# A graph attention layer: which engine loads the last chunks of a quad row by row, and what these loads wait on

## The chip, the core and the metric

The kernel runs on one NeuronCore of a Trainium2 chip. The metric is device time in microseconds (us), as the median of several executions. One further execution was recorded by the hardware profiler; the traces below are from that one.

## What is computed

A graph attention layer over 12,500 nodes with 128 features and 200,000 edges sorted by their target, with 4 heads of 32 values each:

```python
h   = relu(layernorm(x))                        # (12500, 128)
hn  = (h @ W_node.T).reshape(N, 4, 32)
e   = (edge_attr @ W_edge.T).reshape(E, 4, 32)
att = sum(concat([hn[src], hn[tgt], e], -1) * a, -1)   # one score per edge and head
att = where(att > 0, att, 0.2 * att)
m   = maximum(segment_max(att, tgt), 0)
ex  = exp(att - m[tgt])
denom = segment_sum(ex, tgt) + (E - deg)[:, None] * exp(-m)
out = x + segment_sum((ex / denom[tgt])[:, :, None] * hn[src], tgt).reshape(N, 128)
```

The costly access is `hn[src]`: for every edge a row is fetched by the index of its source, and the sources are random.

## The kernel before

**Tiling.** The edges stand in 392 groups of 512 slots (slot 0 of a group carries the sum over from the group before). A group has four chunks of 128 edges, one edge to a partition. Four groups make a quad; there are 98 quads. Quads are joined to "supers": 2 and 2 at the start, 4 in the middle, 3, 3, 2, 2, 2, 2 at the end. A softmax is made once per super.

**The table.** A first stage (until some 97 us) normalizes the nodes, multiplies them by the weights and writes a table to HBM: one row of 137 floats (548 bytes) per node, with the node's values, a one for the count and its scores as a source. Meanwhile GpSimd already gathers raw inputs for the first quads.

**The gathers.** `gather` (L137 to L151) makes one indirect DMA on GpSimd (L149) for each chunk: 128 rows of the table, by the indices in `srci`, to `ga`, a buffer for eight quads. A gather of quad q overwrites what quad q-8 left, so it waits for the matmuls that read that. The gathers of quad q+2 stand in the program at the start of the logits of quad q.

**Chunks by row.** Some chunks aren't gathered on GpSimd. `by_row` (L134) lists quads whose last chunk (group 3, chunk 3) is loaded by ScalarE instead, with 128 separate DMAs of one row each, whose address is taken from a register (`loaded_by_row`, L703 to L725). The registers are loaded from a tile `at_row` of byte offsets, which VectorE makes (L715) from the sources `of` (L708, a load issued by SP), 12 registers at a time (`windows`, L498, a TENSOR_LOAD in the trace). `load_rows` issues a number of these rows at given places: from the sums of quad 6 on, five behind the copy of the count (L756) and one behind the copy of the sums (L759) of each group, so 24 a quad. When the logits of such a quad begin, ScalarE copies the finished tile to `ga` (L870).

**Logits** (`all_logits`, `logits`). For each group VectorE marks which target each edge has (`at`, L558, from the targets `db`), and PE adds the targets' scores (L564, from the windows `pw`) and the edges' (L567, from the features `ea`). Per quad VectorE then adds the sources' scores from the gathered rows (`U`, L588): the first use of a quad's gathers.

**Sums** (`sums`, `complete`, `complete_group`). For each group VectorE weighs the gathered rows (L813) and makes a matrix of marks (L826), and PE sums by target (L833). Then a serial step follows: VectorE scales the sum that runs over from the group before (L752), ScalarE copies its count (L756), PE adds chunk 0 (L758), ScalarE copies the result from PSUM (`pt`, L759). That copy is waited for by L752 of the group after. `divide` (L856, L860) makes the output of a quad, with the inputs `xw`.

**SP's queue.** SP issues the loads `ea` (L310), `db` (L315), `dr` (L540) and, through `issue` (L512), `pw`, `xw` and the stores of the results, in the program's order; an instruction that waits holds all behind it.

**Order.** The order on each engine is written by hand: `together` takes a step of each of several generators in turn. The logits run four to five quads ahead of the sums in mid-kernel, less at the end. The waits are put in by the framework. A DMA issued from SP or ScalarE takes one of eight semaphores (shared by both) and, before it is issued, waits until the DMA that held that semaphore last has landed.

Of the kernel before, what the change touches and what calls it, by code (L numbers as in the profile page):

```python
# [8 lines left out]
F32 = mybir.dt.float32  # L9
BF16 = mybir.dt.bfloat16  # L10
I32 = mybir.dt.int32
# [4 lines left out]
P = 128  # L16
# [10 lines left out]
J = 4  # L27
# [4 lines left out]
QG = 4  # L32
# [18 lines left out]
def kernel(  # L51
# [79 lines left out]
    ga_all = consts.tile([P, QUADS, QG, J, ROW], F32, name="ga")  # L131
    GA, GATHERED = {}, set()
    whole = lambda g: E - g * NE + 1 >= GE
    by_row = [ROWS_FROM + ROWS_AHEAD - -(k + 1) * P // ((BEHIND_COUNT + BEHIND_SUMS) * QG) for k in range(nq)]  # L134
    by_row = [q for q in by_row if q < nq and quads[q][1] == QG and whole(quads[q][0] + QG - 1)]
    is_by_row = lambda q, i, j: q in by_row and (i, j) == (QG - 1, J - 1)

    def gather(q, rows, width, lo, hi):

        g0, m = quads[q]  # L140
        ga = GA[q] = ga_all[:, q % QUADS]
        for i in range(lo, hi):
            n = -(-min(E - (g0 + i) * NE + 1, GE) // P)
            if n < J:
                nc.vector.memset(ga[:, i, n:, :], 0.0)
            for j in range(n):
                if is_by_row(q, i, j):
                    continue
                nc.gpsimd.indirect_dma_start(  # L149
                    out=ga[:, i, j, 0:width], out_offset=None, in_=rows,  # L150
                    in_offset=bass.IndirectOffsetOnAxis(ap=srci[:, g0 + i, j:j + 1], axis=0))  # L151
# [323 lines left out]
    with tc.tile_pool(name="work", bufs=2) as work, \  # L475
# [20 lines left out]
        def windows(of, size, g, n, engine=mybir.EngineType.SP):  # L496

            return nc.values_load_multi_w_load_instructions(  # L498
                of[0:1, g:g + n], engines=[engine], min_val=0, max_val=(N - 1) * size,
                skip_runtime_bounds_check_because="a node's row")[1]  # L500
# [7 lines left out]
        def issue(*kinds, all_of=False):  # L508

            for kind in kinds:  # L510
                for _ in range(len(due[kind]) if all_of else min(1, len(due[kind]))):
                    nc.sync.dma_start(*due[kind].pop(0))  # L512
# [187 lines left out]

        ROW_TILES = {}

        def loaded_by_row():  # L703

            def sources_of(q):
                g = quads[q][0] + QG - 1
                of = work.tile([1, P], I32, name="of")
                nc.sync.dma_start(of, src.rearrange("(o e) -> o e", o=1)[:, (g + 1) * GE - P:(g + 1) * GE])  # L708
                return of

            of = sources_of(by_row[0]) if by_row else None
            yield
            for k, q in enumerate(by_row):
                at_row = work.tile([1, P], I32, name="at_row")
                nc.vector.tensor_scalar(at_row, of, float(4 * ROW), None, op0=OP.mult)  # L715
                tile_q = work.tile([P, ROW], F32, name="by_row")
                for p in range(P):
                    if p == P // 2 and k + 1 < len(by_row):
                        of = sources_of(by_row[k + 1])
                    if p % LOADED == 0:  # L720
                        at = windows(at_row, 4 * ROW, p, min(LOADED, P - p), mybir.EngineType.Activation)
                    nc.scalar.dma_start(as_bytes(tile_q[p:p + 1, :]),  # L722
                                        rows_at(table, at[p % LOADED], 4 * ROW, 1))
                    if p == P - 1:
                        ROW_TILES[q] = tile_q  # L725
                    yield

        def load_rows(q, n):

            for _ in range(n if q >= ROWS_FROM else 0):  # L730
                next(row_steps, None)

        row_steps = loaded_by_row()
        next(row_steps)

        begun, divisions = [], []
        state = {}
# [9 lines left out]
        def complete_group(q, i, ga, hot, pt, acc, fc):  # L747
            g0, m = quads[q]
            g = g0 + i
            if g:  # L750
                before = state["before"]
                nc.vector.tensor_tensor(  # L752
                    ga[0:1, i, 0, 0:H * HW].rearrange("p (h w) -> p h w", w=HW),
                    before[WIN:WIN + 1, 0:H * HW].rearrange("p (h w) -> p h w", w=HW),
                    fc.unsqueeze(2).to_broadcast([1, H, HW]), op=OP.mult)
                nc.scalar.copy(ga[0:1, i, 0, R_CNT:R_CNT + 1], before[WIN:WIN + 1, R_CNT:R_CNT + 1])  # L756
                load_rows(q, BEHIND_COUNT)
            nc.tensor.matmul(acc, hot[:, i, 0, :], ga[:, i, 0, :], start=False, stop=True)  # L758
            nc.scalar.copy(pt[:, i, :], acc)  # L759
            state["before"] = acc  # L760
            load_rows(q, BEHIND_SUMS)
# [28 lines left out]
        def sums(q):  # L790

            for k in range(nq - 3, nq) if q == nq - 3 else [q] if q < nq - 3 else []:
                fetch_inputs(k)
            if q == nq - 4:
                issue("inputs", all_of=True)
            g0, m = quads[q]
            s = of_quad[q]
            s0, sm = groups(s)
            ga = GA.pop(q)
            heads = lambda t: t[:, :, 0:sm * H].rearrange("p j (h g) -> p j h g", h=H)  # L800
            ex, xs, facs = XS[s]
# [64 lines left out]
        def all_logits(q):  # L866
            flush()
            open_logits(q)
            if q in by_row:
                nc.scalar.copy(GA[q][:, QG - 1, J - 1, :], ROW_TILES.pop(q))  # L870
            for i in range(QG):
                logits(q, i)
                issue("weights")
                if i == QG - 1 and q + 2 < nq:
                    issue("weights", all_of=True)
                    fetch_targets(q + 2)
                yield
            state["logits"] = q

# [306 lines left out]
```

## Time and profile before

| what | us |
|---|---|
| median of 3 runs (1998.55 to 2002.2) | 2000.3 |
| the profiled execution | 2004.14 |
| its span, first to last instruction | 2002.4 |
| PE busy, of the span | 1386.6 |
| VectorE busy | 1326.1 |
| ScalarE busy | 420.0 |
| GpSimd busy | 1499.5 |

A row of a group reads: line, engine, operation, what it writes and reads, count; then busy us, mean ns of one; then the idle time of the engine ahead of these instructions and what ended it. In a timeline a row is start us, us, engine, instruction, count, and in brackets the engine's idle time before. "PEld" is the loading of weights in PE, "q" behind an engine's name its sequencer, which issues DMAs and loads registers; these aren't counted as busy.

### The profile page before, as it was taken

The numbers are of one execution on the slowest core, as the hardware profiler recorded it, in microseconds if no ns is written. First come the engines' busy times: TensorE is split into PE (matmuls) and PEld (weight loads), VectorE is DVE, ScalarE is ACT, GpSimd is POOL, SyncE is SP. The second block draws the span as 40 slices with busy tenths as digits, with TensorE's granted clock in tenths as the row PEclk, the third lists the DMA queues.
The fourth block names the chain that finished last, engine by engine and source line by source line (L and its number), as shares of the span: only waits on it lengthen the run. The fifth ranks groups of instructions, "written<-read, shape, count | busy, mean of one in ns | idle before, by whom it ended". The sixth has DMA issues, their size and how long they took to land.

```text
span 2002.4 us, 31260 instructions
## 1 busy us (share of the span) xinstructions
PE 1386.6 (69%) x7327; PEld 1243.7 (62%) x7327; DVE 1326.1 (66%) x3281; ACT 420.0 (21%) x1547; POOL 1499.5 (75%) x1594
## 2 busy tenths in 40 slices
PE   6577877777766757666757675666675766667876
PEld 5567776666665656556656565656564666667775
DVE  6676775776775765655747655656575566667886
ACT  6664111111111111111111111111111111111222
POOL 7777777777777777777777777777777777777774
PEclk8777555555555555555555555555555555555557
DMA  7655765555555554545554555555545565555541
GB/s 252 205 145 118 179 156 134 148 150 150 143 134 140 139 147 123 146 124 135 134 144 125 145 131 131 132 144 124 148 123 144 123 147 127 135 134 139 140 113 37
DMA packets 197514, 279.78 MB, mean 140 GB/s; under 512 B 81544, under 2 KB 146967, under 8 KB 189488
## 3 DMA queue, kind: packets, MB, share of 16 engines
q1 hardware_dynamic: 142158, 165.56, 30.8%
q0 software_dynamic: 49632, 108.56, 23.3%
q10 hardware_dynamic: 5538, 3.64, 0.7%
q8 instruction: 61, 1.00, 0.2%
q14 instruction: 125, 1.02, 0.2%
HBM read 254.26 MB, written 23.30 MB: 139 GB/s over the span
## 4 chain that ended last, share of the span: by engine, by line
DVE 26%; DMA 21%; PE 18%; issue 12%; POOL 11%; ACT 6%; ACTq 4%; SPq 1%; DVEq 0%; POOLq 0%
POOL ga L149 11%; DMA ga<-table,srci 8%; PE acc L833 8%; DVE at L558 4%; PE lg L567 4%; DVE res L860 3%; DMA by_row<-table 3%; ACTq L722 3%; DVE res L856 3%; DMA db<-in_dst_dram 2%; DMA pw<-side 2%; DVE ga L752 2%; DMA ea<-in_edge_t_dram 2%; PE acc L758 2%; DVE ga L813 2%
## 5 line engine op out<-in xcount | busy, mean ns | idle before, releaser
L149 POOL DMA_INDIRECT ga<-table,srci x1479 | 1412.5, 955 | 453.4 <-issue 387.9
L833 PE MATMUL acc<-ga,hot 128*97 128x137 f32 x2352 | 644.4, 445 | 222.0 <-ACT ga L806 184.4
L833 PEld LDWEIGHTS acc<-ga,hot 128*97 128x97 f32 x2352 | 513.4, 276 | 242.4 <-ACT ga L806 195.3
L567 PE MATMUL lg<-wblk,ea 128*128 128x8 f32 x1568 | 405.1, 356 | 0.0
L564 PEld LDWEIGHTS <-at 80*128 80x128 bf16 x1568 | 209.1, 163 | 281.3 <-DVE at L558 259.8
L567 PEld LDWEIGHTS lg<-wblk,ea 128*128 128x128 f32 x1568 | 377.5, 306 | 0.0
L759 ACT COPY pt<-acc 97x137 f32<-97x137 f32 x392 | 107.4, 274 | 1009.9 <-DMA by_row<-table 540.9
L752 DVE TENSOR_TENSOR ga<-acc,facs 1x132 f32<-1x132 f32 x391 | 115.8, 296 | 301.9 <-ACT pt L759 293.7
L564 PE MATMUL lg<-pw,at 80*128 80x12 bf16 x1568 | 169.7, 181 | 210.5 <-DVE at L558 206.4
L758 PE MATMUL acc<-ga,hot 128*97 128x137 f32 x784 | 262.3, 437 | 23.4 <-ACT ga L756 21.5
L558 DVE TENSOR_TENSOR at<-const_ps,db 80x512 bf16<-80x512 f32 x392 | 267.4, 683 | 5.9
L813 DVE TENSOR_TENSOR ga<-ga,ex_ps 128x528 f32<-128x528 f32 x392 | 268.6, 685 | 0.6 <-DVE st L576 0.3
L758 PEld LDWEIGHTS acc<-ga,hot 128*97 128x97 f32 x784 | 190.9, 277 | 44.2 <-ACT ga L756 41.9
L588 DVE TENSOR_TENSOR U<-st,ga 128x64 f32<-128x64 f32 x98 | 26.4, 270 | 243.3 <-DMA ga<-table,srci 213.1
L826 DVE TENSOR_TENSOR hot<-const_ps,slot 128x320 f32<-128x320 f32 x384 | 183.6, 478 | 0.0
L756 ACT COPY ga<-acc 1x1 f32<-1x1 f32 x391 | 59.9, 153 | 193.9 <-DVE ga L752 186.4
L149 POOL DMA_INDIRECT ga<-in_x_dram,srci x72 | 69.1, 959 | 23.1 <-issue 19.8
L856 DVE TENSOR_TENSOR res<-pt,const_ps 80x512 f32<-80x512 f32 (+2 forms) x103 | 67.7, 657 | 4.1 <-DMA pw<-side 0.3
L860 DVE TENSOR_TENSOR res<-res,xw 80x512 f32<-80x512 f32 (+2 forms) x100 | 67.0, 670 | 3.5
L680 PE MATMUL ex_ps<-ident,ex 64*128 64x64 f32 (+2 forms) x112 | 18.2, 310 | 65.6 <-ACT ex L667 65.6
L680 PEld LDWEIGHTS ex_ps<-ident,ex 64*128 64x128 f32 (+2 forms) x112 | 13.4, 202 | 68.3 <-ACT ex L667 68.2
L406 PE MATMUL row_ps<-wcat,hT 128*128 128x137 f32 x198 | 41.4, 361 | 19.3 <-DVE tgt L412 10.0
(139 smaller groups left out, 1041.6 us busy)
## 6 DMA issues: line engine op xcount, KB each, us to landing
db<-in_dst_dram SPq DMA_DIRECT2D x98, 640.0 KB
ea<-in_edge_t_dram SPq DMA_DIRECT2D x98, 512.0 KB
by_row<-table ACTq DMA_DIRECT2D x1920, 0.5 KB
ga<-table,srci POOLq DMA_INDIRECT x1479
xw<-in_x_dram SPq DMA_DIRECT2D x392, 40.0 KB
out_dram<-res SPq DMA_DIRECT2D x392, 40.0 KB
pw<-side SPq DMA_DIRECT2D x392, 1.9 KB
table<-row SPq DMA_DIRECT2D x9, 616.5 KB
```

The lines of the kernel that those rows point to most:

```text
L149: nc.gpsimd.indirect_dma_start(out=ga[:, i, j, 0:width], out_offset=None, in_=rows, in_offset=bass.IndirectOffsetOnAxis(ap=srci[:, g0 + i, ...
L558: nc.vector.tensor_tensor(at[:, i, :], node_ps[0:SPAN, g0 + i:g0 + i + 1].to_broadcast([SPAN, GE]), db[:, i, :], op=OP.is_equal)
L564: nc.tensor.matmul(lg[:, i, j].rearrange("p k h -> p (k h)"), at[:, i, j * P:(j + 1) * P], sw, start=i + j == 0, stop=False, skip_group_ch ...
L567: nc.tensor.matmul(lg[:, i, 2 * w:2 * w + 2, 0, :], ea[:, i, w, :], wblk, start=False, stop=True, skip_group_check=True)
L752: nc.vector.tensor_tensor(ga[0:1, i, 0, 0:H * HW].rearrange("p (h w) -> p h w", w=HW), before[WIN:WIN + 1, 0:H * HW].rearrange("p (h w) -> ...
L758: nc.tensor.matmul(acc, hot[:, i, 0, :], ga[:, i, 0, :], start=False, stop=True)
L759: nc.scalar.copy(pt[:, i, :], acc)
L813: nc.vector.tensor_tensor(val, val, weight.unsqueeze(3).to_broadcast([P, J, H, HW]), op=OP.mult)
L826: nc.vector.tensor_tensor(hot[:, i, :, 0:SPAN], lane_ps.unsqueeze(1).to_broadcast([P, J, SPAN]), slot[:, g, :].unsqueeze(2).to_broadcast([ ...
L833: nc.tensor.matmul(acc, hot[:, i, j, :], ga[:, i, j, :], start=j == 1, stop=False)
L856: nc.vector.tensor_tensor(res[:, :n, :].rearrange("p g (h d) -> p g h d", d=HD), val[:, :, :, 0:HD], share_ps[0:R, :n, :].unsqueeze(3).to_ ...
L860: add.tensor_tensor(res[:, :n, :], res[:, :n, :], xw, op=OP.add)
```

## The change

The rows loaded by ScalarE are 28 a quad instead of 24: after the last group of a quad's sums four more are issued, and the registers are loaded 28 at a time, once per 28 rows. SP loads rows too, 20 a quad, for chunk 2 of group 3 of its own list of quads: three behind each step of the logits and two behind each step of the sums, from quad 2 on, with registers loaded 20 at a time. The list of chunks by row has 31 entries instead of 15. Row tiles have three buffers. Each row DMA adds to one of three semaphores per list that belong to these rows alone, and is left out of the framework's eight; before ScalarE copies a finished tile to `ga`, it waits for the count of that tile's rows.

```diff
-ROWS_FROM, ROWS_AHEAD = 6, 9
-BEHIND_COUNT, BEHIND_SUMS, LOADED = 5, 1, 12
+ROWS_FROM, ROWS_AHEAD, ROW_BUFS = 6, 7, 3
+BEHIND_COUNT, BEHIND_SUMS, BEHIND_QUAD = 5, 1, 4
+SYNC_FROM, BEHIND_LOGITS, BEHIND_HOT = 2, 3, 2
...
-    by_row = [ROWS_FROM + ROWS_AHEAD - -(k + 1) * P // ((BEHIND_COUNT + BEHIND_SUMS) * QG) for k in range(nq)]
-    by_row = [q for q in by_row if q < nq and quads[q][1] == QG and whole(quads[q][0] + QG - 1)]
-    is_by_row = lambda q, i, j: q in by_row and (i, j) == (QG - 1, J - 1)
+    by_row = {}
+
+    def rows_for(a_quad, j, soonest):
+        for k in range(nq):
+            q = soonest - -(k + 1) * P // a_quad
+            if q < nq and quads[q][1] == QG and whole(quads[q][0] + QG - 1):
+                by_row[q, QG - 1, j] = k
+        return a_quad, j
+
+    scalar_rows = rows_for((BEHIND_COUNT + BEHIND_SUMS) * QG + BEHIND_QUAD, J - 1,
+                           ROWS_FROM + ROWS_AHEAD)
+    sync_rows = rows_for((BEHIND_LOGITS + BEHIND_HOT) * QG, J - 2, SYNC_FROM + 6)
...
-                    if p % LOADED == 0:
-                        at = windows(at_row, 4 * ROW, p, min(LOADED, P - p), mybir.EngineType.Activation)
-                    nc.scalar.dma_start(as_bytes(tile_q[p:p + 1, :]),
-                                        rows_at(table, at[p % LOADED], 4 * ROW, 1))
+                    if p % a_quad == 0:
+                        at = windows(at_row, 4 * ROW, p, min(a_quad, P - p), kind)
+                    row = engine.dma_start(as_bytes(to[p:p + 1, :]),
+                                           rows_at(table, at[p % a_quad], 4 * ROW, 1))
+                    row.then_inc(arrived[k % ROW_BUFS], 16)
+                    tc.no_tile_sem_insts.add(row.ins.name)
+                    tc.add_to_no_dep_group(f"rows{q}_{i}_{j}", row.ins)
...
+        def load_rows(steps, q, n):
+            for _ in range(n if q >= (ROWS_FROM if steps is by_scalar else SYNC_FROM) else 0):
+                next(steps, None)
+
+        def take_rows(q):
+            for i, j in [at[1:] for at in by_row if at[0] == q]:
+                to, arrived, count = ROW_TILES.pop((q, i, j))
+                nc.scalar.wait_ge(arrived, count)
+                taken = nc.scalar.copy(GA[q][:, i, j, :], to)
...
+        by_scalar = loaded_by_row(nc.scalar, mybir.EngineType.Activation, *scalar_rows)
+        next(by_scalar)
+        by_sync = loaded_by_row(nc.sync, mybir.EngineType.SP, *sync_rows)
+        next(by_sync)
...
+            if i == m - 1:
+                load_rows(by_scalar, q + 1, BEHIND_QUAD)
...
                 issue("inputs", "results", *(["inputs"] * 3 if q == nq - 3 else []))
+                load_rows(by_sync, q, BEHIND_HOT)
...
-            if q in by_row:
-                nc.scalar.copy(GA[q][:, QG - 1, J - 1, :], ROW_TILES.pop(q))
+            take_rows(q)
...
+                load_rows(by_sync, q, BEHIND_LOGITS)
```

More of the change, by code (lines that the diff above doesn't have):

```diff
@@ L146, in gather @@
             for j in range(n):
-                if is_by_row(q, i, j):
+                if (q, i, j) in by_row:
                     continue
@@ L701, with loaded_by_row, sources_of @@
         ROW_TILES = {}
[L703 to L708, printed above, removed]
+        def loaded_by_row(engine, kind, a_quad, j):
+            chunks = [(q, i) for q, i, c in by_row if c == j]
+            arrived = [tc.alloc_semaphore(f"rows_{j}_{b}") for b in range(ROW_BUFS)]
+            def sources_of(q, i):
+                e = (quads[q][0] + i) * GE + j * P
+                of = work.tile([1, P], I32, name=f"of{j}")
+                nc.sync.dma_start(of, src.rearrange("(o e) -> o e", o=1)[:, e:e + P])
@@ L709, in sources_of @@
                 return of
-            of = sources_of(by_row[0]) if by_row else None
+            of = sources_of(*chunks[0]) if chunks else None
             yield
-            for k, q in enumerate(by_row):
-                at_row = work.tile([1, P], I32, name="at_row")
+            for k, (q, i) in enumerate(chunks):
+                at_row = work.tile([1, P], I32, name=f"at_row{j}")
                 nc.vector.tensor_scalar(at_row, of, float(4 * ROW), None, op0=OP.mult)
-                tile_q = work.tile([P, ROW], F32, name="by_row")
+                to = work.tile([P, ROW], F32, name=f"by_row{j}", bufs=ROW_BUFS)
@@ L717, in loaded_by_row @@
                 for p in range(P):
-                    if p == P // 2 and k + 1 < len(by_row):
-                        of = sources_of(by_row[k + 1])
-                    if p % LOADED == 0:
-                        at = windows(at_row, 4 * ROW, p, min(LOADED, P - p), mybir.EngineType.Activation)
-                    nc.scalar.dma_start(as_bytes(tile_q[p:p + 1, :]),
-                                        rows_at(table, at[p % LOADED], 4 * ROW, 1))
+                    if p == P // 2 and k + 1 < len(chunks):
+                        of = sources_of(*chunks[k + 1])
@@ L724, in loaded_by_row @@
+                    if p % a_quad == 0:
[5 more added lines that the diff above has]
+                    tc.add_to_no_dep_group(f"rows{q}_{i}_{j}", row.ins)
                     if p == P - 1:
-                        ROW_TILES[q] = tile_q
+                        ROW_TILES[q, i, j] = to, arrived[k % ROW_BUFS], 16 * P * (k // ROW_BUFS + 1)
@@ L726, in loaded_by_row @@
                     yield
[L728 to L734, printed above, removed]
+        def load_rows(steps, q, n):
[6 more added lines that the diff above has]
+                taken = nc.scalar.copy(GA[q][:, i, j, :], to)
+                tc.declare_no_dep(taken.ins, group=f"rows{q}_{i}_{j}",
+                                  reason="a semaphore counts the rows of this chunk")
+                tc.declare_fence(taken.ins, group=f"rows{q}_{i}_{j}")
@@ L756, in complete_group @@
                 nc.scalar.copy(ga[0:1, i, 0, R_CNT:R_CNT + 1], before[WIN:WIN + 1, R_CNT:R_CNT + 1])
-                load_rows(q, BEHIND_COUNT)
+                load_rows(by_scalar, q, BEHIND_COUNT)
             nc.tensor.matmul(acc, hot[:, i, 0, :], ga[:, i, 0, :], start=False, stop=True)
@@ L760, in complete_group @@
             state["before"] = acc
-            load_rows(q, BEHIND_SUMS)
+            load_rows(by_scalar, q, BEHIND_SUMS)
             parts = {nq - 1: (2, 3), nq - 2: (2,), nq - 3: (2,), nq - 4: (2,)}.get(q, ())
```

## The prediction

> **What bounds the kernel now.** I read the page's groups first, then busy time by stage, then what the consumers wait for. A quad is four groups of 512 edge slots, so 16 chunks of 128 edges; there are 98 quads.
>
> ```profile
> L149 POOL DMA_INDIRECT ga<-table,srci x1479 | 1412.5, 955 | 453.4 <-issue 387.9
> L149 POOL DMA_INDIRECT ga<-in_x_dram,srci x72 | 69.1, 959 | 23.1 <-issue 19.8
> ```
> ```profile
> POOL ga L149 <- issue: 407.7, 1336, 0.3
> ```
>
> GpSimd gathers one chunk per instruction. One gather with the gap before it takes (1412.5 + 453.4) / 1479 = 1.262 us. The second fence is of the waits (us in total, times, longest): the gaps come 1336 times from issuing alone and the longest is 0.3 us. So GpSimd issues without a pause.
>
> ```profile
> 1958.64 0.95 POOL L149 DMA_INDIRECT ga<-table,srci  x1 [0.30 <-issue]
> 1959.62 0.51 POOL L786 TENSOR_SCALAR hot<-lane,slot 128x80 f32<-128x80 f32 x1
> ```
>
> The last gather ends at 1958.64 + 0.95 = 1959.6 us; 42.8 us of the span of 2002.4 follow. Is somebody waiting for these gathers? VectorE's add of the gathered scores (U, L588, once a quad) is their first reader.
>
> ```profile
> DVE U L588 <- DMA ga<-table,srci: 210.9, 51, 8.4
> ```
> ```profile
> 262.48 0.27 DVE L588 TENSOR_TENSOR U<-st,ga 128x64 f32<-128x64 f32 x1
> ```
> ```profile
> 531.72 0.27 DVE L588 TENSOR_TENSOR U<-st,ga 128x64 f32<-128x64 f32 x1
> ```
>
> The first row is of the stretch from 527 to 1724 us: 51 of its 60 quads wait for a gather. Before that stretch the consumers, who began late, catch up: quads 10 to 25 took (531.72 - 262.48) / 15 = 17.9 us each, against about 16 x 1.262 = 20.2 us of gathers. No other engine is full:
>
> ```profile
> 3.00:527.00 524.00, 387.82 (x2134) 346.41 (x2135) 370.71 (x1061) 176.84 (x549) 395.36 (x415) 0.61 0.61 162
> 527.00:1724.00 1197.00, 795.33 (x4128) 714.57 (x4127) 746.98 (x1713) 186.42 (x766) 907.62 (x949) 0.51 0.55 136
> 1724.00:1960.00 236.00, 177.22 (x922) 160.49 (x923) 179.12 (x420) 46.30 (x189) 178.94 (x189) 0.53 0.52 129
> 1960.00:2002.40 42.40, 26.24 (x144) 22.22 (x144) 28.76 (x83) 10.48 (x44) 16.58 (x35) 0.74 0.11 30
> ```
>
> Columns: stretch, its length, busy us of PE, PE loads, VectorE, ScalarE, GpSimd, then PE's granted clock, DMA share, GB/s. In the second stretch VectorE is busy 62%, the DMA engines 55%. (GpSimd's 76% leaves out its issue gaps.) The gather count sets the time, up to the last hundred or two microseconds.
>
> **The change, part by part.**
>
> *Gathers removed.* Before, 15 chunks go by rows (1920 / 128). After, ScalarE's chunk k stands in quad 13 + ceil(128(k+1)/28), which is at most 97 for 18 chunks; SP's in quad 8 + ceil(128(k+1)/20), for 13. That makes 31, so 16 gathers fewer: 16 x 1.262 = **20.2 us** off the gather stream. Up to quad 85 it is 27 against 13, so 14 fewer, 17.7 us; up to quad 95, 15 fewer, 18.9 us.
>
> *What is late next.* From quad 86 the consumers trail the gathers on their own account:
>
> ```profile
> 1728.18 0.27 DVE L588 TENSOR_TENSOR U<-st,ga 128x64 f32<-128x64 f32 x1 [3.72 <-issue]
> 1759.45 0.27 DVE L588 TENSOR_TENSOR U<-st,ga 128x64 f32<-128x64 f32 x1
> ...
> 1925.64 0.27 DVE L588 TENSOR_TENSOR U<-st,ga 128x64 f32<-128x64 f32 x1 [1.86 <-DMA ga<-table,srci]
> 1944.75 0.27 DVE L588 TENSOR_TENSOR U<-st,ga 128x64 f32<-128x64 f32 x1
> 1961.69 0.27 DVE L588 TENSOR_TENSOR U<-st,ga 128x64 f32<-128x64 f32 x1 [0.31 <-DMA ga<-table,srci]
> ```
> ```profile
> 1742.38 0.95 POOL L149 DMA_INDIRECT ga<-table,srci  x1 [0.30 <-issue]
> ```
>
> These are quads 85, 86, 95, 96, 97; the gather, counted in order of issue, is quad 86's last. It ends at 1743.3; the add starts 16 us later and waits for nothing; only at quad 95 does the add wait again. So the add of 86 comes 17.7 us earlier. At 95 the old wait of 1.86 us can go, but the gather allows 18.9. At 97 a further 0.31 can go: **19.2 us** reach the last add. The 40.7 us behind it stay as they are: no row is loaded there, before or after.
>
> *ScalarE's rows.* A row's issue:
>
> ```profile
> L722 ACTq DMA_DIRECT2D by_row<-table x1920: 227/234/589, 266.2 to 1816.9; - x192
> ```
> ```profile
> 1001.75 1.58 ACTq L722 DMA_DIRECT2D by_row<-table  x5
> ```
> ```profile
> 1012.10 1.64 ACTq L722 DMA_DIRECT2D by_row<-table  x5
> ...
> 1016.26 3.72 ACTq L722 DMA_DIRECT2D by_row<-table  x5
> ```
> ```profile
> L498 ACTq TENSOR_LOAD <-at_row x165: 725/1059/1175, 265.1 to 1810.6; - x165
> L498 SPq TENSOR_LOAD <-base_side x98: 293/304/587, 98.9 to 1906.1; - x98
> ```
>
> Five rows take 1.6 us undisturbed, so 0.33 each with the register move between. The burst of 3.72 us is the old wait: each row DMA reused one of eight semaphores and stood until that semaphore's last DMA, SP's included, had landed. With semaphores of their own the rows lose it. Per quad: 4 rows more, 1.3 us. A load of 12 registers takes 1.06 us, of 4 (SP) 0.30, so some 0.095 per register and about 2.6 us for 28; 90 loads x 2.6 replace 165 x 1.06, over 82 and 80 quads 2.8 us against 2.2. Together about 2 us more per quad, against what the waits give back. In the stretch from 527 to 1724 all this lies beside the gathers: the consumers need 17.9 us against 19.8 after. The cover is 1.9 us per quad; beyond it every microsecond per quad would cost about 60.
>
> *The end of the rows.* ScalarE's 2304 rows: 4 behind sums 5, 28 each in sums 6 to 85 (2240), and 60 left for sums 86 to 88, where before there were none and where the consumers pace themselves.
>
> ```profile
> ACT pt L759 <- DMA by_row<-table: 41.3, 13, 5.0
> ```
> ```profile
> ACT pt L759 <- PE acc L758: 20.3, 12, 2.1
> ```
>
> The first is of 1728 to 1819 us (sums 81 to 85, with rows), the second of 1819 to 1862 (sums 86 to 88, without). Without rows ScalarE waits 20.3 / 12 = 1.7 us a group for PE before it copies pt, just what five rows take: they are hidden. Not hidden are two or three loads (2.6 each) and the four rows at a quad's end: 5 to 10 us. From the first row comes relief: 41.3 - 13 x 1.64 = 20 us above clean bursts, about half of it the loads, which remain. I take the two as equal, 0; bounds: 10 us gained (of which the gathers pass only 1.0), 27 us lost if nothing hides (60 x 0.33 + 3 x 2.6).
>
> *SP's rows.* No trace shows a row on SP. The nearest rows:
>
> ```profile
> L512 SPq DMA_DIRECT2D pw<-side x392: 317/369/1864, 99.5 to 1919.4; - x196
> ...
> L512 SPq DMA_DIRECT2D xw<-in_x_dram x392: 317/363/1818, 137.6 to 1967.5; - x196
> ...
> L512 SPq DMA_DIRECT2D out_dram<-res x392: 316/340/1229, 166.0 to 1999.0; - x196
> ```
>
> Bounds per row: 0.33 as on ScalarE, 0.40 as an SP issue of 0.37 with its move; I take 0.33, as the transfer is the same. Twenty are 6.6 us a quad, the loads (91 of up to 20 registers, about 1.9) 2.1 us. SP's own work is 4 x (0.37 + 0.36 + 0.34 + 0.09) + 1.5 for ea, db and loads, about 6.1. That makes 15 of 19.8 us. Queued behind the rows are pw, xw, db, ea and the results. The targets db are the tightest of the loads that logits need:
>
> ```profile
> 1002.39 0.32 SPq L315 DMA_DIRECT2D db<-in_dst_dram  x1
> ```
> ```profile
> 1030.27 0.68 DVE L558 TENSOR_TENSOR at<-const_ps,db 80x512 bf16<-80x512 f32 x1
> ```
>
> In mid-kernel that is 28 us from issue to use, for a transfer of 640 KB: a few microseconds of SP's rows ahead of it are hidden. Cost taken: 0. The room is least early, in the logits of quads 6 and 7:
>
> ```profile
> 214.33 0.32 SPq L315 DMA_DIRECT2D db<-in_dst_dram  x1
> ```
> ```profile
> 222.72 0.68 DVE L558 TENSOR_TENSOR at<-const_ps,db 80x512 bf16<-80x512 f32 x1
> ```
> ```profile
> 242.15 0.66 PE L758 MATMUL acc<-ga,hot 128*97 128x137 f32 x2
> ```
> ```profile
> 247.05 0.95 POOL L149 DMA_INDIRECT ga<-table,srci  x1 [0.30 <-PE lg L567]
> ```
>
> Quad 8's db is issued 8.1 us before its use. Quad 12's first gather starts 247.05 - 242.81 = 4.2 us after the matmul that frees its buffer: the smallest such room among quads 8 to 29, each first gather set against its own matmul. If SP's rows make early consumers over 4 us later, GpSimd waits and the excess is lost for good.
>
> *The copies.* 16 more of about 0.3 us on ScalarE, one every five quads: nothing.
>
> **Sum.** The profiled execution took 2004.14 us (span 2002.4): 2004.1 - 19.2 = 1984.9. The median of the three runs, 2000.3, lies 3.8 lower: **1981.1 us**.
>
> **Rivals.**
>
> *The consumers become the bound at the end.* Sums 86 to 88 pay 8 us for loads and leftover rows and the relief fails: 1981.1 + 8 = 1989; bound 1981.1 + 27 = 2008. For it: nothing there waits for gathers. Against: the 1.7 us under PE, and the 41.3 us that shrink ahead of it.
>
> *GpSimd stalls early.* SP runs 8 us behind near 215 us, db lands late; less the room of 4.2, 4 us are lost: 1985.
>
> *Slower: ScalarE and SP exclude each other while issuing.* If a row holds the shared path for its whole 0.33 us, a quad asks for 48 x 0.33 + 14.3 x 0.36 = 21.0 us, more than the 20.2 of now, over some 83 quads: 66 us later than before, 2066. It decides from (19.8 - 5.1) / 48 = 0.31 us per row up. With only the recorded 0.234 it would be 16.4 us, and hidden. Against it: SP's issue of db at 1002.39 us (quoted above) fell inside ScalarE's burst of 1.58 us from 1001.75; the burst from 1012.10, with no issue of SP inside, took 1.64. Had they excluded each other, it would show some 0.3 us more.
>
> The Trainium skill (Perfetto Trace Analysis, "DMA Instruction — HWDGE (DVE, Sync)") says that the block which generates the descriptors is shared by the two sequencers and is locked for exclusive use while one generates. By that rule this rival would hold if the lock filled the whole spacing; the trace's burst speaks for a short hold.
>
> *It doesn't do what it says.* Rows still wait somewhere (a chunk late, ScalarE held at its copy). SP's chunk is issued some four quads ahead of its use, ScalarE's two: unlikely. It would take back the gain: about 2000.
>
> **How the numbers follow.** Chances: forecast (1977 to 1984) 0.67; consumers late at the end 0.13; early stall 0.08; rows late 0.05; slower by exclusion or an SP row far above 0.40 us, 0.07. About 0.2%, 4 us, is what a measurement here can tell. Faster by more than that: the first three nearly whole, 0.86. Same: 0.05. Slower: 0.09, with the bound of the end. Range 1976 to 1994: from the last gather gaining all 20.2 us with a few microseconds of tail and of run to run, to the end phase losing somewhat more than I priced.
>
> **What would show it.** Right: 1535 gathers, still 1.26 us each with no gap over 0.3; last gather near 1939; no wait of pt on row DMAs beyond 1.7 us but for loads; SP's row near 0.33 apart. Wrong: gaps on GpSimd near 250 us (early stall); adds of quads 86 to 97 without waits and more than 5 us behind their gathers (end phase); row spacing over 0.4 us where both issue (exclusion); mid-kernel adds no longer waiting for gathers.

## The result, and the profile after

| | before | after |
|---|---|---|
| median of 5 runs each, us | 1999.37 (1997.89 to 2002.2) | 1982.21 (1978.93 to 1988.17) |
| ratio, 95% interval | | 0.9916 [0.9896, 0.9935] |
| the profiled execution, its span, us | 2004.14, 2002.4 | 1978.93, 1976.9 |

The forecast was 1981.1 us (1976 to 1994). The changed kernel is 17.2 us faster by the medians. The profiled executions lie 25.2 us apart, since that of before was 3.8 us above the median of the three runs known to the prediction (4.8 above that of the five here), and that of after was the fastest of its five; this matters below.

The groups of the gathers in the changed kernel (line, engine, operation, count; busy us, mean ns; idle us before them):

```profile
L160 POOL DMA_INDIRECT ga<-table,srci x1463 | 1391.9, 951 | 448.1 <-issue 389.2
...
L160 POOL DMA_INDIRECT ga<-in_x_dram,srci x72 | 68.8, 956 | 23.1 <-issue 18.3
```

1463 + 72 = 1535 gathers, and one with its gap takes (1391.9 + 448.1) / 1463 = 1.2577 us. What was waited for (us in total, times, longest):

```profile
ACT pt L788 <- PE acc L787: 539.1, 309, 4.7
POOL ga L160 <- issue: 407.5, 1336, 0.3
...
DVE U L599 <- DMA ga<-table,srci: 241.3, 42, 10.4
...
DVE res L892 <- DMA xw<-in_x_dram: 41.1, 17, 4.8
```

GpSimd still stands only for issuing, 0.3 us at most. VectorE's add of the scores (U) still waits for gathers. ScalarE's copy of pt now waits for PE; in the kernel before the first entry was a wait for row DMAs:

```profile
ACT pt L759 <- DMA by_row<-table: 540.9, 199, 5.3
```

The last row of the fence ahead of it is new: the outputs wait for xw, an input that SP loads, now that rows stand ahead of it in SP's queue. The last gather and the last add of scores, from the timeline:

```profile
1932.53 0.94 POOL L160 DMA_INDIRECT ga<-table,srci  x1 [0.31 <-issue]
```
```profile
1935.73 0.40 DVE L599 TENSOR_TENSOR U<-st,ga 128x64 f32<-128x64 f32 x1 [0.48 <-DMA ga<-table,srci]
```

The gathers end at 1933.5 us, before at 1959.6: 26.1 us earlier. The add starts 26.0 us earlier. Behind the last gather come 1976.9 - 1933.5 = 43.4 us, before 42.8. So the whole gain stands in the stream of gathers, and the stages around it look as they did (columns as in the prediction):

```profile
3.00:527.00 524.00, 384.20 (x2139) 346.17 (x2140) 373.38 (x1071) 178.47 (x554) 395.44 (x416) 0.61 0.62 163
527.00:1700.00 1173.00, 794.00 (x4115) 715.58 (x4114) 745.88 (x1717) 190.18 (x773) 888.54 (x933) 0.50 0.56 138
1700.00:1934.00 234.00, 179.70 (x934) 162.43 (x934) 180.12 (x423) 47.32 (x192) 177.24 (x188) 0.51 0.53 133
1934.00:1976.80 42.80, 27.00 (x144) 22.88 (x144) 29.30 (x83) 10.49 (x44) 16.42 (x35) 0.74 0.11 28
```

In the second stretch GpSimd is busy 888.54 / 1173 = 76%, as before, VectorE 64% and the DMA engines 56%: of these, none but GpSimd came near to full. The queues of SP and ScalarE, where the new rows stand, aren't among these columns; they are weighed below.

Where do 26.1 us come from, if 16 gathers were removed? 16 x 1.2616 = 20.2. The other 6 are 1535 x (1.2616 - 1.2577) = 6.0: each gather was 4 ns shorter in this execution. Whether the change had a part in that stays open; experiment e12 comes back to it.

### The profile page after: what moved, and what is told of

It is laid out like the page before. It is cut to its first block, busy times and chain, and to the rows that moved or that the text cites. A ratio compares the mean times of both kernels' runs of the same rounds, so it can differ in the third digit from the quotient of the medians.

```text
span 1976.9 us, 35316 instructions
## 1 busy us (share of the span) xinstructions
PE 1384.9 (70%) x7327; PEld 1247.0 (63%) x7327; DVE 1329.2 (67%) x3297; ACT 426.4 (22%) x1563; POOL 1478.6 (75%) x1578
## 5 line engine op out<-in xcount | busy, mean ns | idle before, releaser
L160 POOL DMA_INDIRECT ga<-table,srci x1463 | 1391.9, 951 | 448.1 <-issue 389.2
L575 PEld LDWEIGHTS <-at 80*128 80x128 bf16 x1568 | 213.7, 164 | 384.0 <-DVE at L569 362.2
L417 PEld LDWEIGHTS row_ps<-wcat,hT 128*128 128x128 f32 x198 | 33.0, 239 | 26.8 <-ACT hn L248 16.6
```

What stands on the lines that cost most here:

```text
L160: nc.gpsimd.indirect_dma_start(out=ga[:, i, j, 0:width], out_offset=None, in_=rows, in_offset=bass.IndirectOffsetOnAxis(ap=srci[:, g0 + i, ...
L417: nc.tensor.matmul(row_ps[:, t, :ROW], hT[:, t, :], wcat, start=True, stop=True)
L575: nc.tensor.matmul(lg[:, i, j].rearrange("p k h -> p (k h)"), at[:, i, j * P:(j + 1) * P], sw, start=i + j == 0, stop=False, skip_group_ch ...
```

## The experiments

Three theories were put to the test. *Theory 1*: the count of gathers sets the time; rows, waits and copies are hidden. *Theory 2*: the gain comes from ScalarE, whose rows lost their waits. *Theory 3*: SP's rows cost time of their own, since inputs come late behind them.

A word on the chips. Three runs (e5, e6, e12) fell on one chip where the kernel before took 1999.4 and 2003.1 us, as it did for the prediction; it is called the chip of the prediction below, though whether it is the same one isn't known. The other nine fell on three further chips, where the kernel before itself took 2552 to 2597 us. Each ratio is taken against the kernel before on the same chip; what those nine tell is a matter of its own, at the end.

### e12: only the gathers removed

The kernel before, with its rows, semaphores and loads untouched; 16 chunks are not gathered. Their buffers keep what was there eight quads earlier, so this part of the computation is left out.

```diff
     is_by_row = lambda q, i, j: q in by_row and (i, j) == (QG - 1, J - 1)
+    left_out = [8 - -(k + 1) * P // 20 for k in range(13)]
+    is_left_out = lambda q, i, j: (i, j) == (QG - 1, J - 2) and q in left_out or (i, j) == (QG - 2, J - 1) and q in (32, 68, 96)
...
-                if is_by_row(q, i, j):
+                if is_by_row(q, i, j) or is_left_out(q, i, j):
                     continue
```

> The kernel before with its 1920 rows, semaphores and loads as they are, in which 16 more chunks are simply not gathered (SP's 13 of the changed kernel and three more, so that 14 are gone by quad 85, 15 by quad 95 and 16 at the end): 1535 gathers, no row added. Those 16 chunks keep what their buffer held eight quads earlier: that part of the computation is left out. Where the kernel before takes about 2000 us: theory 1 (the count of gathers sets the time, the change's rows and waits are hidden) 19.2 us less, ratio 0.990, the changed kernel's 0.992 within 0.002. Theory 2 (the change gained by ScalarE's rows losing their waits) 1998 to 2001, ratio 1.00. Theory 3 (the rows that SP issues cost time of their own, that the changed kernel pays) below the changed kernel by over 4 us, ratio under 0.990. Where the kernel before takes 2550 to 2600 us, SP and ScalarE pace the kernel and the gathers are not what it waits for: ratio 0.999 to 1.001, which would show that gathers saved are worth nothing there.

Measured: 1982.21 us (1981.09 to 1986.59) against 2003.09, ratio 0.9896 [0.9878, 0.9914]. Its waits, and the groups and timeline rows of its last gather and last add:

```profile
ACT pt L761 <- DMA by_row<-table: 580.3, 209, 5.0
```
```profile
POOL ga L151 <- issue: 406.3, 1332, 0.3
```
```profile
L151 POOL DMA_INDIRECT ga<-table,srci x1463 | 1399.8, 957 | 446.9 <-issue 388.0
```
```profile
1939.67 1.40 POOL L151 DMA_INDIRECT ga<-table,srci  x1 [0.30 <-issue]
```
```profile
1944.02 0.34 DVE L590 TENSOR_TENSOR U<-st,ga 128x64 f32<-128x64 f32 x1
```

ScalarE waits for row DMAs as long as ever (580.3 us in 209 waits), and the time falls all the same. **Theory 2 falls**: those waits were hidden before, and the whole gain comes without their going. **Theory 1 holds**: the count alone is enough for it. Against theory 3, the interval of e12 overlaps those of the change (0.9916 [0.9896, 0.9935] here, 0.9922 [0.9906, 0.9937] in e5), and the medians in us are the same to 0.2. The point values leave 2.0 to 2.6 thousandths, some 4 to 5 us, that the rows may cost. I can't find them in the traces, where GpSimd doesn't wait in either kernel and the stretch behind the last gather is 43.4 us in the one and 1984.8 - 1941.1 = 43.7 in the other. They stay open.

The group's row also bears on the 6 us above. Here a gather takes (1399.8 + 446.9) / 1463 = 1.2623 us, and the profiled execution, 1986.59 us, was the slowest of its four. So 1535 gathers cost 1.2577 us each in one trace and 1.2623 in another, which is 7 us in all, about the spread of the runs. Two readings fit this. Both traces of the changed kernel (the one above and e5's, 1.2571) have the shorter gathers and were the fastest of their five runs; both traces without SP's rows (before and e12) have the longer ones and were slower than all other runs of theirs. The medians speak for a difference between executions, since they show a gain of 17 us and not of 26; but no kernel was profiled twice in executions of clearly different length, so it isn't shown.

### e5 and e6: the change again, and with 28 rows a quad on SP

e5 is the changed kernel as it is. e6 has four rows behind each step of the logits and three behind each of the sums, with registers loaded 28 at a time: 37 chunks by row, 1529 gathers.

```diff
-SYNC_FROM, BEHIND_LOGITS, BEHIND_HOT = 2, 3, 2
+SYNC_FROM, BEHIND_LOGITS, BEHIND_HOT = 2, 4, 3
```

> The changed kernel itself once more. In the first four experiments the kernel before took 2585 us, not 2000, on their chip: there the sequencers of SP and ScalarE stood still for some 0.7 us every few instructions (register moves of up to 1.4 us, 0.03 in the first traces), and GpSimd waited for matmuls. Where the kernel before takes about 2000 us, theory 1 (the number of gathers sets the time): 15 to 20 us faster, gaps on GpSimd no longer than 0.32 us. Where it takes about 2585 us, theory 4 (what SP and ScalarE issue sets the time there): 4 to 8% slower than before, as with SP's rows and all gathers kept (ratio 1.069), since 13 gathers fewer are worth nothing while GpSimd waits.

> The change with 28 rows a quad on SP instead of 20 (four behind a step of the logits, three behind one of the sums, 28 registers a load): 37 chunks by row, 1529 gathers, 6 fewer than the change. Where the kernel before takes about 2000 us: theory 1 alone gives 6 x 1.26 = 7.6 us less than the change, some 25 us faster than before. A rival: SP, now with about 28 x 0.33 + 1.5 x 2 + 6 = 18 us of a quad of 19.7, falls behind, xw and db come late and GpSimd waits in the early quads, where the room is 1.7 us in the change: no faster than the change or slower. Where the kernel before takes about 2585 us: slower than the change by 2% or more.

Measured, on one chip with before at 1999.36: e5 1982.05 (1977.33 to 1987.33), ratio 0.9922 [0.9906, 0.9937]. e6 2051.66 (2047.81 to 2059.25), ratio 1.0274 [1.0251, 1.0296]. Six gathers fewer than the change, and 70 us slower.

The trace of e6 shows the start of it: the targets of quad 8 (db) come late behind SP's rows, VectorE stands, and the first gather that needs a freed buffer stands too.

```profile
230.92 0.69 DVE L569 TENSOR_TENSOR at<-const_ps,db 80x512 bf16<-80x512 f32 x1 [9.07 <-DMA db<-in_dst_dram]
```
```profile
251.47 0.94 POOL L160 DMA_INDIRECT ga<-table,srci  x1 [5.88 <-PE acc L787]
```

From there on the consumers don't catch up. The adds of quads 10 to 25, in e6 and then in the changed kernel (count, and first and last start):

```profile
L599 DVE TENSOR_TENSOR U<-st,ga x16: 266/267/270, 278.3 to 575.9; 128x64 f32<-128x64 f32 x16
```
```profile
L599 DVE TENSOR_TENSOR U<-st,ga x16: 266/267/271, 267.0 to 530.6; 128x64 f32<-128x64 f32 x16
```

That is (575.9 - 278.3) / 15 = 19.8 us a quad against 17.6. The gathers of e6 need 1529 / 98 x 1.257 = 19.6, so a lag can't shrink. What the outputs wait for in e6:

```profile
DVE res L892 <- DMA xw<-in_x_dram: 243.4, 50, 8.0
...
DVE res L892 <- DMA pw<-side: 75.2, 13, 7.8
```

And SP's longest wait, in total, between 672 and 1702 us (52 quads):

```profile
SPq L523 <- DMA out_dram<-res: 17.5, 20, 1.9
```

All of SP's waits in that stretch make 45 us, 0.9 a quad: SP is all but full, at 19.8 us a quad. The end:

```profile
1945.16 0.94 POOL L160 DMA_INDIRECT ga<-table,srci  x1 [0.30 <-issue]
```
```profile
2004.87 0.26 DVE L599 TENSOR_TENSOR U<-st,ga 128x64 f32<-128x64 f32 x1
```

The last gather ends at 1946.1, 13.7 us later than in e5 (1932.4), since GpSimd waited for buffers; and the last add comes 58.8 us behind it, where the change has 2.3. 13.7 and 56.5 make 70 of the 72.4 us between the spans (2047.6 and 1975.2). So **theory 3 is true eight rows further on**: the change stands short of that edge, how far is worked out below.

### e1 and e9: the semaphores alone; e2: ScalarE's rows alone

Undone: SP's rows, and for e1 and e9 (the same kernel on two chips) also ScalarE's four more rows and the long loads: 24 rows a quad, 15 chunks, 1551 gathers.

```diff
-ROWS_FROM, ROWS_AHEAD, ROW_BUFS = 6, 7, 3
-BEHIND_COUNT, BEHIND_SUMS, BEHIND_QUAD = 5, 1, 4
-SYNC_FROM, BEHIND_LOGITS, BEHIND_HOT = 2, 3, 2
+ROWS_FROM, ROWS_AHEAD, ROW_BUFS = 6, 9, 3
+BEHIND_COUNT, BEHIND_SUMS, BEHIND_QUAD = 5, 1, 0
+SYNC_FROM, BEHIND_LOGITS, BEHIND_HOT = 2, 0, 0
+LOADED = 12
...
-                    if p % a_quad == 0:
-                        at = windows(at_row, 4 * ROW, p, min(a_quad, P - p), kind)
+                    if p % LOADED == 0:
+                        at = windows(at_row, 4 * ROW, p, min(LOADED, P - p), kind)
...
```

> ScalarE alone loads rows, 24 a quad and 12 registers at a time as before (15 chunks by row, 1551 gathers); only the semaphores are those of the change. Theory 1 (the number of gathers sets the time): last gather near 1955 to 1960 us into the span, and the median within 3 us of before, although pt's wait on row DMAs (540.9 us before) goes; at most 2 us can be had at quads 95 and 97, where the adds wait for gathers. Theory 2 (the gain came from ScalarE's waits that go): 12 to 18 us faster than before with the same number of gathers.

> Only the semaphores of the change: 24 rows a quad on ScalarE as before (15 chunks, 1551 gathers, loads of 12), no rows on SP, each buffer of rows counted on a semaphore of its own. Where the kernel before takes about 2000 us: theory 1 (the count of gathers sets the time) 2000 within 3 us, although ScalarE's waits on row DMAs are gone. Theory 2 (ScalarE's waits were part of the bound) 1982 to 1992. Where the kernel before takes about 2585 us: the same as before, ratio 1.00.

e2 keeps ScalarE's 28 rows and loads (18 chunks, 1548 gathers) and has no rows on SP:

```diff
-SYNC_FROM, BEHIND_LOGITS, BEHIND_HOT = 2, 3, 2
+SYNC_FROM, BEHIND_LOGITS, BEHIND_HOT = 2, 0, 0
...
-    sync_rows = rows_for((BEHIND_LOGITS + BEHIND_HOT) * QG, J - 2, SYNC_FROM + 6)
+    sync_rows = 20, J - 2
```

> ScalarE's part of the change alone: 28 rows a quad, own semaphores, no rows on SP (18 chunks by row, 1548 gathers). Theory 1: 3 gathers fewer, 3 x 1.26 = 3.8 us faster than before (1 to 6). Theory 2: 12 to 18 us faster, as the change.

Measured: e1 2589.29 against 2585.10, ratio 1.0017 [0.9998, 1.0036]; e9 2549.70 against 2552.42, 0.9993 [0.9972, 1.0014]; e2 2598.46 against 2585.10, 1.0052 [1.0037, 1.0067]. These are chips where the kernel before itself takes 28 to 29% longer. Own semaphores alone change nothing there; e2, with four rows a quad more, longer loads and three gathers fewer, takes 0.5% longer, where 1 to 6 us less had been expected. What either does on the chip of the prediction wasn't measured.

### e3, e7 and e11: all rows, but SP's chunks gathered too

The rows of the change; SP's 13 chunks are gathered as well, and their rows are copied to a tile that nobody reads (1548 gathers). It was to separate the theories; all three runs fell on the other chips.

```diff
-                if (q, i, j) in by_row:
+                if (q, i, j) in by_row and j == J - 1:
...
-                taken = nc.scalar.copy(GA[q][:, i, j, :], to)
+                taken = nc.scalar.copy(GA[q][:, i, j, :] if j == J - 1 else unread, to)
```

> All rows of the change are loaded, but SP's 13 chunks are gathered by GpSimd as well; SP's finished tiles are copied to a tile that nobody reads, behind the same waits. 1548 gathers, as with ScalarE's rows alone. Theory 1: the same time as that kernel, 2 to 6 us faster than before: SP's rows are hidden. Theory 2: as the change, some 17 us faster. Theory 3 (SP's rows cost time of their own, by xw or db that come later): slower than ScalarE's rows alone by 3 us or more.

> All rows of the changed kernel are issued as there, but SP's 13 chunks are also gathered by GpSimd (their rows are copied to a tile that nobody reads): 1548 gathers. Where the kernel before takes about 2000 us on this chip: theory 1 (the count of gathers sets the time, the rest is hidden) 13 x 1.26 = 16.4 us above the changed kernel's 1982, so about 1998, ratio 0.999. Theory 2 (the gain came from ScalarE's rows losing their waits, gathers matter little): 1982 to 1985. Theory 3 (SP's rows cost time of their own): above 2001. Where the kernel before takes about 2585 us, the sequencers of SP and ScalarE bound the kernel, and 6 to 7% above it is expected again.

> All rows of the changed kernel are issued as there, but SP's 13 chunks are also gathered by GpSimd (their rows are copied to a tile that nobody reads): 1548 gathers. Where the kernel before takes about 2000 us on this chip: theory 1 (the count of gathers sets the time, the rest is hidden) 13 x 1.26 = 16.4 us above the changed kernel's 1982, so about 1998, ratio 0.999. Theory 2 (the gain came from ScalarE's rows losing their waits, gathers matter little): 1982 to 1985. Theory 3 (SP's rows cost time of their own): above 2001. Where the kernel before takes about 2550 to 2585 us, SP and ScalarE pace the kernel, and 6 to 7% above it is expected again.

Measured: 2766.11 us, ratio 1.0687 [1.0645, 1.0729]; 2711.53, 1.0608 [1.0576, 1.0640]; 2785.78, 1.0731 [1.0703, 1.0759]. It says nothing on the theories for the chip of the prediction.

### e4 and e8: the framework's semaphores; e10: SP's rows from quad 14

In e4 and e8 the whole change is made (1535 gathers), but the row DMAs take the framework's eight semaphores in turn. In e10 SP's rows begin at quad 14. Its trace shows 1465 + 72 = 1537 gathers and 29 copies of finished tiles, so 29 chunks by row, not the 30 that were expected.

```diff
-            arrived = [tc.alloc_semaphore(f"rows_{j}_{b}") for b in range(ROW_BUFS)]
...
-                    row = engine.dma_start(as_bytes(to[p:p + 1, :]),
+                    engine.dma_start(as_bytes(to[p:p + 1, :]),
                                            rows_at(table, at[p % a_quad], 4 * ROW, 1))
-                    row.then_inc(arrived[k % ROW_BUFS], 16)
...
```
```diff
-SYNC_FROM, BEHIND_LOGITS, BEHIND_HOT = 2, 3, 2
+SYNC_FROM, BEHIND_LOGITS, BEHIND_HOT = 14, 3, 2
```

> The change with all its rows (1535 gathers), but each row DMA takes one of the framework's eight semaphores, as before, and waits for that semaphore's last DMA. Strict theory 1: 17 to 20 us faster than before, as the change: waits of ScalarE and SP are hidden. Theory 2: no faster than before. By the rows of before, a row lands some 2 to 4 us after its issue and 62 DMAs a quad share eight semaphores: 62 / 8 x 2.5 = 19 us of a quad of 19.8, so SP and ScalarE would be nearly full; I expect between 20 us faster and 60 us slower, and pt's wait on row DMAs far over 540.9 us.

> The whole change with 1535 gathers, but the row DMAs use the framework's shared semaphores again, each reused in turn, in place of their own. Where the kernel before takes about 2000 us: theory 1 (only the count of gathers matters, waits of ScalarE and SP are hidden) 1982, as the changed kernel. Theory 2 (own semaphores are what makes it work, since 28 and 20 rows a quad that stand for a landed DMA do not fit into 19.8 us): a row then costs some 0.5 to 0.7 us instead of 0.33 on both queues, so 48 rows ask 24 to 34 us of the two queues and the consumers fall behind in mid-kernel: 2030 to 2200, adds of mid-kernel without waits for gathers. Where the kernel before takes about 2585 us: 13% above it as before.

> The change with SP's rows beginning at quad 14 instead of 2 (30 chunks by row, 1536 gathers, one more than the changed kernel), so that the early quads, in which SP fell 10 us behind and quad 12's first gather had 1.7 us of room left, are as before. Where the kernel before takes about 2000 us: theory 1 (early lag hidden, count sets the time) 1.26 us above the changed kernel's 1982, so 1983 within 3, with quad 12's room back near 4 us. Theory 3 (the early lag costs time in some executions, which would make the spread of 1977 to 1988) 1978 to 1980 and a spread under 6 us. Where the kernel before takes about 2585 us: 5 to 7% above it.

Measured: e4 2932.53, ratio 1.1345 [1.1315, 1.1375]; e8 2886.44, 1.1304 [1.1272, 1.1336]; e10 2672.24, 1.0474 [1.0444, 1.0504], a little under the 5 to 7% that had been expected. On those chips the shared semaphores cost a further 166 us (e4 against e3) and 175 us (e8 against e7), though they go with 13 gathers fewer. Whether the change would work with them on the chip of the prediction, and whether a later start of SP's rows would help there, wasn't measured.

### What the other three chips have in common

In e9, GpSimd's wait for matmuls that free its buffers, the register moves ahead of ScalarE's rows (ns: least, median, most), and a burst of five rows:

```profile
POOL ga L161 <- PE acc L788: 170.7, 39, 23.3
```
```profile
L737 ACTq MOVE by_row<-table x1920: 2/29/1387, 399.6 to 2328.8; - x192
```
```profile
1016.44 2.90 ACTq L737 DMA_DIRECT2D by_row<-table  x5
```

And the same moves in the changed kernel on the chip of the prediction:

```profile
L736 ACTq MOVE by_row<-table x2304: 29/29/38, 271.3 to 1823.2; - x192
```

A move takes 29 ns on both, but here no more than 38, and there up to 1387. Counted over the whole trace of e9, 104 moves on ScalarE and 228 on SP take over 100 ns, 70 and 140 us together; in the changed kernel not one does. The gathers are no slower there (e9: median 947 ns, as before). So on those chips the queues of ScalarE and SP lose time at many instructions, and GpSimd waits for buffers: the consumers set the pace there, by this reading since they hang on these queues. Rows cost time there. What a gather saved is worth there isn't shown: e10 is 39 us faster than e7 on the same chip, with 11 gathers and 256 rows fewer. In e11:

```profile
POOL ga L160 <- PE acc L789: 483.7, 90, 22.2
```
```profile
DVE res L894 <- DMA xw<-in_x_dram: 285.3, 38, 13.7
```

Why these queues stall was not found, and the changed kernel itself wasn't run there. The nearest to it is e10, the change with two chunks by row fewer, which takes 4.7% longer than the kernel before; so I expect the change to be slower than before on such a chip. That is argued, not shown.

## Why the prediction was right, point by point

**The gather stream: right.** 16 x 1.262 = 20.2 us was forecast, with the last gather near 1939 us. In the profiled execution it ended at 1933.5, 26.1 us earlier than before: 20.2 by the count, and 6 by shorter gathers, for which the forecast had no term. Of the 19.2 that were to reach the last add, the medians show 17.2, with an interval of 13 to 21 from the ratio; that the median fell 1.1 us from the forecast is closer than this interval can vouch for. e12, which removes nothing but gathers, gives 20.8 (17 to 24).

**From the profiled execution to the median: right to take it off.** The 3.8 us are of the size by which the gathers differ from trace to trace (7 us between the change and e12).

**The end of the quads: right in the sum, the size within the bounds.** The consumers were to lose nothing. They gained. Quad 86, its last gather and its add:

```profile
1719.52 0.94 POOL L160 DMA_INDIRECT ga<-table,srci  x1 [0.30 <-issue]
```
```profile
1729.05 0.27 DVE L599 TENSOR_TENSOR U<-st,ga 128x64 f32<-128x64 f32 x1
```
```profile
1899.48 0.27 DVE L599 TENSOR_TENSOR U<-st,ga 128x64 f32<-128x64 f32 x1 [4.48 <-DMA ga<-table,srci]
```

The add comes 8.6 us behind its gather, before 16. The relief outweighed the 60 rows by 7.5 us, inside the bound of 10; at quad 95 (last row) the add waits 4.48 us for its gather, so as forecast the surplus isn't passed on. The rival "consumers bound at the end" is out. That the relief doesn't come from the gathers, e12 shows, where they go and the waits for row DMAs stay. Quad 86's last gather and its add there:

```profile
1725.90 0.95 POOL L151 DMA_INDIRECT ga<-table,srci  x1 [0.30 <-issue]
```
```profile
1743.45 0.27 DVE L590 TENSOR_TENSOR U<-st,ga 128x64 f32<-128x64 f32 x1
```

That is 16.6 us, as before. So the waits weren't hidden everywhere: at the end they held the consumers back, which the wait for the gathers of quad 95 then covered. One step was too cautious: 1.0 of the 20.2 us was to stop at the last adds, while in the traces the last add moved as far as the last gather (26.0 and 26.1 us).

**ScalarE's rows: right in effect, the load mis-sized.** Loads of registers:

```profile
L509 SPq TENSOR_LOAD <-base_side x98: 297/492/574, 97.8 to 1877.2; - x98
L509 SPq TENSOR_LOAD <-base_row x98: 294/561/627, 137.1 to 1934.7; - x98
L509 SPq TENSOR_LOAD <-at_row x91: 526/1448/1632, 128.8 to 1718.9; - x91
L509 ACTq TENSOR_LOAD <-at_row x90: 1190/1981/2182, 269.3 to 1815.4; - x90
```

28 registers take 1.98 us where I had drawn the line from 4 and 12 on to 2.6; 20 take 1.45, not 1.9. Beyond 12, a further register costs 0.05 to 0.07 us, not 0.095. On the other hand SP's old loads of 4 went from 0.30 to 0.49 and 0.56 us, which I had not counted. The forecast that nothing of this shows held: quads 10 to 25 took 17.6 us, before 17.9.

**SP's rows: the row right, the budget too low, the cover thinner than said.** A row: median 234 ns recorded, as on ScalarE.

```profile
L736 ACTq DMA_DIRECT2D by_row<-table x2304: 227/235/542, 271.4 to 1823.3; - x192
...
L736 SPq DMA_DIRECT2D by_row<-table x1664: 227/234/922, 130.1 to 1728.7; - x185
```

I had SP's quad at 15 us. e6 has eight rows more and loads of 28, which is 8 x 0.33 + 0.43 = 3.1 us a quad; with its 0.9 us of waits taken off the 19.8, 20 rows need about 15.8. The changed kernel's own trace agrees. From 672 to 1702 us, 52 quads, SP's longest wait in total is

```profile
SPq L523 <- DVE res L892: 159.1, 46, 6.0
```

and all its waits make 190 us, 3.6 of 19.7 a quad, which leaves 16.0 of work. The step that was mis-sized is SP's old work. In the kernel before, SP waits 628 us in the same stretch, 12.1 of 19.9 a quad, which leaves 7.8; I had summed 6.1, so 1.7 us too little, of which the loads, half a microsecond shorter than forecast, gave some back. The cost, 0, stood because a quad had 1535 / 98 x 1.2577 = 19.7.

**The early room: the place right, a near miss.** The rival "GpSimd stalls early" named quad 8's targets and quad 12's first gather. In the changed kernel:

```profile
220.10 0.37 SPq L326 DMA_DIRECT2D db<-in_dst_dram  x1
```
```profile
224.47 0.69 DVE L569 TENSOR_TENSOR at<-const_ps,db 80x512 bf16<-80x512 f32 x1 [2.67 <-DMA db<-in_dst_dram]
```
```profile
243.91 0.66 PE L787 MATMUL acc<-ga,hot 128*97 128x137 f32 x2
```
```profile
246.30 0.95 POOL L160 DMA_INDIRECT ga<-table,srci  x1 [0.31 <-PE acc L864]
```

SP issues db 5.8 us later than before, VectorE waits 2.67 us for it, and the gather that needs the buffer (its 0.31 is the gap that every gather has) starts 246.30 - 244.57 = 1.7 us behind the matmul that frees it: 4.2 shrank to 1.7, and in e5 to 1.1. No time was lost, by so little; the forecast had no size for this, only a chance, so that it held was in part luck. In e6 the very gather waited 5.88 us.

**Exclusion while issuing: right to reject.** Two bursts of ScalarE; then three rows of SP that end inside the second, and a load of `xw` inside it:

```profile
1001.26 1.54 ACTq L736 DMA_DIRECT2D by_row<-table  x5
...
1005.35 1.54 ACTq L736 DMA_DIRECT2D by_row<-table  x5
```
```profile
1004.85 0.93 SPq L736 DMA_DIRECT2D by_row<-table  x3
1006.20 0.32 SPq L523 DMA_DIRECT2D xw<-in_x_dram  x1
```

1.54 us with SP silent, 1.54 with SP issuing. Over the whole trace, 1463 of ScalarE's 2304 rows overlap an issue of SP by more than half and 661 not at all: the median issue is 235 ns in both, the mean 248 and 240. The shared path that the Trainium skill describes (Perfetto Trace Analysis, "DMA Instruction — HWDGE (DVE, Sync)"), locked for exclusive use while it generates descriptors, shows next to no price here.

**"It doesn't do what it says": out.** 31 chunks left the gathers, 1535 against 1551 with 15, and pt waits for no row DMA any more. ScalarE's idle time ahead of the 31 copies of finished tiles is small:

```profile
ACT ga L755 <- issue: 42.3, 29, 3.4
```

That is 1.5 us each, about what five rows ahead in its queue would take; no chunk held it for longer than 3.4 us.

## What to carry to other kernels

Find the one stream that issues without a pause, count its instructions, and multiply: e12 shows that the count alone carried this gain, while 540 us of waits elsewhere could stay without costing any of it. Work that is moved to idle queues is free only while each queue's whole load per unit stays under the bounding stream's. Read the load that a queue already has from its waits in the trace: the sum of its instructions was 1.7 us of 7.8 short here. The edge matters, since eight rows too many turned 17 us of gain into 52 us of loss. Look for the tightest buffer at the start, where the consumers begin late: what was lost there in e6 was never caught up, since the paces were equal.

## What the runs showed of the hardware

- The same gathers took 1.2571 to 1.2623 us each in four profiled executions of three kernels, a difference of some 8 us over 1535; the two shorter figures are both of the changed kernel.
- Loading 4, 12, 20 and 28 registers took 0.30 (SP), 1.06 (ScalarE), 1.45 (SP) and 1.98 us (ScalarE); a load of 4 on SP went to 0.49 and 0.56 us once rows were loaded there.
- On three of the chips the queues of SP and ScalarE stalled, up to 1.4 us at a register move of 29 ns, and the kernel before took 2552 to 2597 us instead of 2000. The change is worth 0.8% on one chip; two chunks by row short of it, in e10, the kernel took 4.7% longer than before on another.
